# Layer 0's attention: scaling the second product by GpSimd in SBUF instead of by VectorE out of PSUM

## The chip, the cores and the metric

The kernel runs on one core of one Trainium2 chip. The metric is the device time of one execution in microseconds (us); the median of a few runs is compared. The profile is one execution taken apart by the hardware profiler. Its engines are PE (TensorE matmuls), PEld (TensorE weight loads), DVE (VectorE), ACT (ScalarE), POOL (GpSimd) and SP (SyncE, which issues most DMA transfers).

## The reference

Two layers follow each other on x of shape (8, 512, 32, 32): 8 images, 512 channels, T = 1024 pixels, all fp32. Each is a group norm, 1x1 convolutions to q, k and v, softmax attention over the pixels, a 1x1 projection, and the residual sum. Layer 0 has 8 heads of 64 channels, layer 1 one head of 512. The change is in layer 0's attention:

```
h = group_norm(x)
q, k, v = split(w_qkv @ h + b_qkv)            # per head: 64 channels x 1024 pixels
weight = softmax(q^T k / sqrt(64))            # over s, the 1024 source pixels
a[c, t] = sum_s weight[t, s] * v[c, s]
out = x + w_proj @ a + b_proj
```

The kernel leaves the division of the softmax to the end: e = exp(score), a = (sum_s e v) / (sum_s e). So a needs two things for every column t: the unscaled product, and the reciprocal of the column's sum.

## The kernel before, in words

**Work over the images.** One loop runs over the 8 images b. Each pass has the attention of layer 0 for image b (`attention0`, line 395), then a stage of products (v of the next image, projection of this one, q and k of the next), then layer 1 for image b. Products of 512 x 512 by 512 x 1024 are made in seven half-size products instead of eight (`wino`, line 223), for which VectorE makes sums and differences of halves (`left_sums`, `right_sums`; the lines 155 to 158 and 166 to 169). The tiles `t_h` and `h` of the next image get theirs during `attention0`, through the list `extra`; the tile `a` gets its own (`image_factors(a)`, tiles `t_a`) after it.

**attention0.** It handles 8 blocks per image: 4 head pairs `hp`, and for each the two halves `tb` of 512 target pixels. A block has 8 steps s over 128 source pixels each. In a step, TensorE makes the two heads' scores `sc` (128 x 1024 in PSUM, two banks; three such buffers rotate), ScalarE takes the exponential into a tile `e` (line 413), and VectorE adds `e` into the tile `sum` (called `total` in the code; line 415 for the first add, line 417 for six more). Then TensorE makes `av`, the product of `e` with `v`: 16 matmuls into one PSUM bank, head 0 in partitions 0 to 63 and head 1 in 64 to 127.

**reciprocals** (line 366). Four small matmuls with a matrix of ones add `sum` over the partitions (`sums`, in PSUM). VectorE takes the reciprocal `rc` (line 377) and keeps the least one seen (`low_recs`, line 378); GpSimd adds all of them up in `all_recs` (line 379); both serve a check at the kernel's end. The values lie in a compact form, so SP writes them to DRAM as rows (line 381) and reads them back twice, one row for each head, spread over 64 partitions each, into the tile `r` (line 391).

**Scaling.** The function `scaled` multiplies `av`, in PSUM, by `r` and writes `a`:

```python
                    def scaled(hp=hp, tb=tb, av=av, r=r):
                        nc.vector.tensor_mul(a[hp][:, ts(tb, HT)], av, r)
```

It is called in the next block, after that block's adds in the program. The last block's `scaled` is handed to the caller, which calls it in the stage of products.

**Buffers.** `av` and `sums` share a PSUM pool of two banks (`acc_tile`). `rc` and `r` have two SBUF buffers each (`rpool`). A buffer is given out again when its last reader is done.

**Order.** The order of each engine's instructions is fixed at compile time by the tile framework, which plays the program through with a cost model and places what it holds ready; matmuls alone are kept in program order. At run time each engine takes its instructions in that fixed order, each when its semaphores allow.

Of the kernel before, what the change touches and what calls it, by code (L numbers as in the profile page):

```python
# [12 lines left out]
ALU = mybir.AluOpType  # L13
# [15 lines left out]
def two_attention_blocks_kernel(  # L29
# [8 lines left out]
    nc = tc.nc  # L38
    B, C, T = x.shape
    KC = C // P  # L40
    HT = T // 2
# [23 lines left out]
    def matmul(*args, **kw):  # L65
        tc.keep_in_program_order(nc.tensor.matmul(*args, **kw))  # L66
# [105 lines left out]
    def main_path(ctx):  # L172
# [11 lines left out]
        def pair_tile(name):  # L184
            return big_tile(name, (P, 2, HT))

        def acc_tile(name):
            return ps_acc.tile([P, HT], F32, tag="acc", name=name)
# [168 lines left out]
        def channel_tiles(name):  # L357
            return [big_tile(f"{name}_{c}") for c in range(KC)]
# [7 lines left out]
        def reciprocals(total, uid, across):  # L366

            sums = acc_tile(f"sums_{uid}")[:, : 2 * P].rearrange("p (a b) -> p a b", a=2)
            for i in range(4):
                matmul(sums[ts(i, 32), :, :], ones[:, :32], total[:, :, ts(i, P)], start=True, stop=True)
            rc = rpool.tile([P, 2, P], F32, tag="rc", name=f"rc_{uid}")
            nc.vector.reciprocal(rc, sums)  # L377
            nc.vector.tensor_tensor(low_recs, low_recs, rc, ALU.min)
            nc.gpsimd.tensor_tensor(all_recs, all_recs, rc, ALU.add)  # L379
            rows = rowpool.tile([2, 4, P], F32, tag="rows", name=f"rows_{uid}")  # L380
            nc.sync.dma_start(rows.rearrange("j i n -> i j n"), rc[0:P:32, :, :])
            if across:
                r = pair_tile(f"r_{uid}")
                for j in range(2):
                    row = rows[j : j + 1].rearrange("j i n -> j (i n)")
                    nc.sync.dma_start(r[:, j, :], row.to_broadcast([P, HT]))
            else:
                r = rpool.tile([P, HT], F32, tag="r", name=f"r_{uid}")
                for j in range(2):
                    row = rows[j : j + 1].rearrange("j i n -> j (i n)")  # L390
                    nc.sync.dma_start(r[ts(j, 64), :], row.to_broadcast([64, HT]))
            return r


        def attention0(b, q, k, v, extra):
            a = channel_tiles(f"a0_{b}")
            scaled = None
            n = 0
            for hp in range(KC):
                for tb in range(2):  # L400
                    uid = f"0_{b}_{hp}_{tb}"
                    total = pair_tile(f"sum_{uid}")
                    es = []
                    for s in range(NS):
                        sc = ps_pools[n % 3].tile([P, 2, HT], F32, tag="sc", name=f"sc_{uid}_{s}")
                        n += 1
                        for j in range(2):
                            matmul(
                                sc[:, j, :], k[hp][ts(j, 64), ts(s, P)], q[hp][ts(j, 64), ts(tb, HT)],
                                start=True, stop=True,  # L410
                            )
                        e = pair_tile(f"e_{uid}_{s}")
                        nc.scalar.activation(e, sc, AF.Exp, scale=(C // 8) ** -0.5)  # L413
                        if s == 1:
                            nc.vector.tensor_add(total, es[0], e)  # L415
                        elif s > 1:
                            nc.vector.tensor_add(total, total, e)  # L417
                        es.append(e)
                    for f in extra.pop(0) if extra else ():
                        f()  # L420
                    if scaled:
                        scaled()
                    av = acc_tile(f"av_{uid}")
                    for s in range(NS):
                        for j in range(2):
                            matmul(
                                av[ts(j, 64), :], v[s // 2][:, s % 2, hp * P + j * 64 : hp * P + (j + 1) * 64],
                                es[s][:, j, :], start=(s == 0), stop=(s == NS - 1),
                            )
                    for f in extra.pop(0) if extra else ():  # L430
                        f()
                    r = reciprocals(total, uid, False)

                    def scaled(hp=hp, tb=tb, av=av, r=r):
                        nc.vector.tensor_mul(a[hp][:, ts(tb, HT)], av, r)  # L435

            assert not extra
            return a, scaled
# [165 lines left out]
        for b in range(B):  # L604
# [5 lines left out]
            if more:  # L610
# [4 lines left out]
                for i, f in enumerate(steps):  # L615
                    extra[8 + i].append(f)
            psum_pools(f"attention_{b}", 1)
            a, scaled = attention0(b, q, k, v, extra)
            psum_pools(f"products_{b}", 2)

# [309 lines left out]
```

## Time and profile before

| what | value |
| --- | --- |
| time, three runs | 2998.86, 3001.4 and 3006.32 us, median 3001.4 |
| the profiled execution | 3001.43 us; its span, first to last instruction, 2998.6 us |
| granted TensorE clock | 0.994 |
| busy in the span: PE, DVE, ACT, POOL | 98%, 61%, 25%, 4% |
| one block of `attention0` when nothing is late | 14.65 us |
| blocks in the program | 64 (8 images, 8 each) |
| `e` (ACT, line 413) | 512 times, mean 1.051 us |
| `sum` adds (DVE, line 417) | 384 times, mean 1.223 us |
| `a<-av,r` (DVE, line 435) | 64 times, mean 0.686 us |
| `all_recs` add of 128 x 256 (POOL, line 379) | 72 times, mean 0.883 us |

Busy time is a sum over the whole span. A block's 14.65 us are read in the timeline as the distance from its first score matmul to the next block's. The seven windows of the images 2 to 8 from the first score matmul of their attention to the first `sums` matmul of its last block or a little later show 90.5 us of DVE work in about 115 us, 59.5 of ACT and 6.3 of POOL.

### The profile page before, as it was taken

Reading aid. Unit: us, or ns where it says so; the run is one execution under the profiler, and the core shown is the slowest. Engines: PE = TensorE matmul, PEld = TensorE weight load, DVE = VectorE, ACT = ScalarE, POOL = GpSimd, SP = SyncE. Lnnn points to the kernel's source line nnn. Section 1 sums busy time; section 2 is a strip of 40 time slices with the busy share of each in tenths; the row PEclk is TensorE's granted clock in tenths of the full one; section 3 lists DMA queues with packets and bytes.
Section 4 is the critical chain, followed back from the end, with each engine's and each line's share of the span. In section 5 each row is a group of like instructions: output and inputs, shape, how many; then the busy total and the mean of one; then the engine's idle time right before and its main releaser. Section 6 shows DMA issues by size and latency. Waiting matters only on the chain.

```text
span 2998.6 us, 26895 instructions
## 1 busy us (share of the span) xinstructions
PE 2944.2 (98%) x10322; PEld 1409.5 (47%) x10322; DVE 1836.1 (61%) x2445; ACT 754.6 (25%) x925; POOL 112.8 (4%) x119
## 2 busy tenths in 40 slices
PE   7999999999999999999999999999999999999899
PEld 5535454354543545435453354534445354543345
DVE  4376565764667647575466754677546765557745
ACT  1153111421124111341114411143111431214220
POOL 0000000000000000000000000000000000000000
PEclk9999999999999999999999999999999999999899
DMA  7422314023140231402322133411324023030100
GB/s 258 166 80 80 138 60 172 19 92 130 59 169 18 107 142 51 150 27 100 144 101 96 47 115 113 145 46 46 130 105 168 19 76 140 33 144 19 39 0 37
DMA packets 78296, 283.56 MB, mean 95 GB/s; under 512 B 9360, under 2 KB 16336, under 8 KB 71632
## 3 DMA queue, kind: packets, MB, share of 16 engines
q1 hardware_dynamic: 77744, 281.61, 26.3%
q8 instruction: 83, 1.36, 0.2%
q14 instruction: 53, 0.43, 0.0%
q10 hardware_dynamic: 416, 0.16, 0.0%
HBM read 207.51 MB, written 74.22 MB: 94 GB/s over the span
## 4 chain that ended last, share of the span: by engine, by line
PE 84%; DVE 7%; issue 4%; DMA 3%; ACT 1%; SPq 0%; POOL 0%; DVEq 0%; ACTq 0%; POOLq 0%
PE sc L66 9%; PE av L66 8%; PE psb_av L66 5%; PE psb_sc L66 5%; DVE sum L417 5%; PE psa_av L66 4%; PE psc_av L66 4%; PE psc_sc L66 4%; PE psa_sc L66 4%; PE psb_z L66 3%; PE psb_q L66 3%; PE psb_v L66 3%; PE psb_g L66 3%; PE psb_k L66 3%; PE psb_p L66 2%
## 5 line engine op out<-in xcount | busy, mean ns | idle before, releaser
L413 ACT ACTIVATE e<-sc 128x1024 f32<-128x1024 f32 x512 | 476.4, 1051 | 582.7 <-PE sc L66 582.7
L417 DVE TENSOR_TENSOR sum<-sum,e 128x1024 f32<-128x1024 f32 x384 | 469.8, 1223 | 34.5 <-ACT e L413 0.8
L66 PE MATMUL sc<-q_again,k_again 64*128 64x512 f32 x1792 | 399.7, 596 | 0.0
L66 PE MATMUL av<-e,v_again 128*64 128x512 f32 x1792 | 396.9, 595 | 0.0
L66 PEld LDWEIGHTS sc<-q_again,k_again 64*128 64x128 f32 x1792 | 166.7, 186 | 212.2 <-ACT e L413 103.7
L66 PEld LDWEIGHTS av<-e,v_again 128*64 128x64 f32 x1792 | 123.7, 137 | 266.3 <-issue 254.2
L377 DVE RECIPROCAL rc<-sums 128x256 f32<-128x256 f32 x72 | 126.4, 1756 | 80.3 <-PE sums L66 47.7
L379 POOL TENSOR_TENSOR all_recs<-all_recs,rc 128x256 f32<-128x256 f32 x72 | 63.6, 883 | 1611.1 <-DVE rc L377 1611.1
L464 ACT ACTIVATE e<-e 128x512 f32<-128x512 f32 x96 | 60.3, 630 | 238.8 <-DVE e L463 238.8
L66 PE MATMUL psa_sc<-g,h 128*128 128x512 f32 x256 | 115.1, 592 | 0.0
L66 PE MATMUL psa_av<-e,z 128*128 128x512 f32 x256 | 113.2, 595 | 0.0
L415 DVE TENSOR_TENSOR sum<-e,e 128x1024 f32<-128x1024 f32 x64 | 78.4, 1225 | 48.9 <-ACT e L413 48.9
L136 ACT ACTIVATE h<-h,b,s 128x1024 f32<-128x1024 f32 x30 | 36.5, 1238 | 169.3 <-DMA h<-in_x 161.4
L66 PEld LDWEIGHTS psa_sc<-g,h 128*128 128x128 f32 x256 | 48.6, 190 | 61.2 <-issue 61.2
L66 PEld LDWEIGHTS psa_av<-e,z 128*128 128x128 f32 x256 | 48.0, 190 | 54.8 <-issue 50.6
L435 DVE TENSOR_TENSOR a<-av,r 128x512 f32<-128x512 f32 x64 | 43.9, 686 | 46.2 <-DMA r<-rows 46.2
L234 DVE TENSOR_TENSOR u_av<-psb_av,t_av 128x512 f32<-128x512 f32 x16 | 11.1, 691 | 93.1 <-PE psb_av L66 93.1
L66 PE MATMUL psb_p<-t_a,w_p 128*128 128x512 f32 x128 | 60.5, 615 | 5.2 <-DVE t_a L167 5.2
L66 PE MATMUL sums<-sum,ones 128*32 128x256 f32 x576 | 46.0, 391 | 18.1 <-DVE sum L417 17.9
L66 PE MATMUL psa_g<-h,w_m 128*128 128x512 f32 x128 | 60.0, 613 | 3.2 <-ACT h L136 3.2
L66 PE MATMUL sc<-q,k 64*128 64x512 f32 x256 | 59.2, 612 | 0.7 <-ACT e L413 0.7
L66 PE MATMUL psb_z<-w_z,t_h 128*128 128x256 f32 x256 | 58.4, 381 | 0.0
(281 smaller groups left out, 4159.1 us busy)
## 6 DMA issues: line engine op xcount, KB each, us to landing
x<-in_x SPq DMA_DIRECT2D x36, 512.0 KB
h<-in_x SPq DMA_DIRECT2D x32, 512.0 KB
r<-rows SPq DMA_DIRECT2D x128, 128.0 KB
out<-x SPq DMA_DIRECT2D x64, 256.0 KB
w_p<-sums_p SPq DMA_DIRECT2D x8, 1792.0 KB
spill<-v SPq DMA_DIRECT2D x28, 512.0 KB
w_m<-sums_m SPq DMA_DIRECT2D x8, 1792.0 KB
spill<-q SPq DMA_DIRECT2D x28, 512.0 KB
```

The lines of the kernel that those rows point to most:

```text
L66: tc.keep_in_program_order(nc.tensor.matmul(*args, **kw))
L136: nc.scalar.activation(dst, src, AF.Identity, bias=b, scale=s)
L234: nc.vector.tensor_add(t[i], ps["b", i], t1[i])
L377: nc.vector.reciprocal(rc, sums)
L379: nc.gpsimd.tensor_tensor(all_recs, all_recs, rc, ALU.add)
L413: nc.scalar.activation(e, sc, AF.Exp, scale=(C // 8) ** -0.5)
L415: nc.vector.tensor_add(total, es[0], e)
L417: nc.vector.tensor_add(total, total, e)
L435: nc.vector.tensor_mul(a[hp][:, ts(tb, HT)], av, r)
L464: nc.scalar.activation(dst, dst, AF.Exp, scale=scale)
```

## The change

ScalarE copies `av` out of PSUM into `a` as soon as the product is there, unscaled. When `r` has come through DRAM, GpSimd multiplies that half of `a` by `r` in place, in SBUF, for the first seven blocks of an image. For the last block of an image the multiplication stays with VectorE and with the caller, now in place in SBUF. The reciprocals, their rows in DRAM and the loads of `r` stay as they are.

```diff
         def attention0(b, q, k, v, extra):
             a = channel_tiles(f"a0_{b}")
-            scaled = None
             n = 0
...
                     for f in extra.pop(0) if extra else ():
                         f()
-                    if scaled:
-                        scaled()
                     av = acc_tile(f"av_{uid}")
...
                     for f in extra.pop(0) if extra else ():
                         f()
+                    dst = a[hp][:, ts(tb, HT)]
+                    nc.scalar.copy(dst, av)
                     r = reciprocals(total, uid, False)
-
-                    def scaled(hp=hp, tb=tb, av=av, r=r):
-                        nc.vector.tensor_mul(a[hp][:, ts(tb, HT)], av, r)
+                    if (hp, tb) != (KC - 1, 1):
+                        nc.gpsimd.tensor_tensor(dst, dst, r, ALU.mult)
+                    else:
+                        scaled = lambda dst=dst, r=r: nc.vector.tensor_mul(dst, dst, r)
```

## Prediction, made before the result was known

> **What bounds the kernel now.** I read the page's busy table first.
>
> ```profile
> span 2998.6 us, 26895 instructions
> PE 2944.2 (98%) x10322; PEld 1409.5 (47%) x10322; DVE 1836.1 (61%) x2445; ACT 754.6 (25%) x925; POOL 112.8 (4%) x119
> ```
>
> TensorE is busy for 2944.2 us: only 54.4 us are idle, and no change to other engines can win more than that. So the question is which idle time of TensorE the changed multiplication causes. The view of the tile `a` shows how long VectorE stood still in front of it:
>
> ```profile
> L435 DVE TENSOR_TENSOR a<-av,r x64: 678/684/693, 173.9 to 2810.7; 128x512 f32<-128x512 f32 x64
> its engine sat idle before it (us, times) until:
>   DMA r<-rows: 46.2, 27
> ```
>
> Idle VectorE costs nothing by itself. The view of line 417 says who waited for the adds queued behind it:
>
> ```profile
> who waited for it (us, times):
>   PEld sums L66: 39.2, 24
>   PE sums L66: 17.9, 23
> ```
>
> TensorE's `sums` matmuls came late 23 times, 17.9 us in all. The timeline of the fifth block of image 3 shows one such case, VectorE first, then TensorE:
>
> ```profile
> 935.55 1.23 DVE L415 TENSOR_TENSOR sum<-e,e 128x1024 f32<-128x1024 f32 x1 [0.74 <-ACT e L413]
> 936.88 1.23 DVE L417 TENSOR_TENSOR sum<-sum,e 128x1024 f32<-128x1024 f32 x1
> 939.55 0.69 DVE L435 TENSOR_TENSOR a<-av,r 128x512 f32<-128x512 f32 x1 [1.45 <-DMA r<-rows]
> 940.16 5.20 DVE L417 TENSOR_TENSOR sum<-sum,e 128x1024 f32<-128x1024 f32 x4
> 945.28 1.29 DVE L166 TENSOR_TENSOR t_h<-h 128x512 f32<-128x512 f32 x2
> 946.49 1.22 DVE L417 TENSOR_TENSOR sum<-sum,e 128x1024 f32<-128x1024 f32 x1
> ```
>
> ```profile
> 939.47 7.09 PE L66 MATMUL av<-e,v_again 128*64 128x512 f32 x32
> 947.75 0.64 PE L66 MATMUL sums<-sum,ones 128*32 128x256 f32 x8 [1.20 <-DVE sum L417]
> ```
>
> The multiplication was placed behind two adds, its row came 1.45 us too late, five adds stood behind it, and the last ended at 947.71. TensorE had been through with `av` at 939.47 + 7.02 = 946.49 (in a block without delay `sums` starts 7.02 after `av`). The same timeline for all 64 blocks gives a fixed pattern: the start of `sums` less that of `av`, less 7.02, is zero in the blocks 1, 2, 4, 6 and 8 of every image and positive in 3, 5 and 7, where the multiplication sits early; in the others it is the last or last but one before the final add, and the row has long landed. Summed over the images: 4.0 us in the third blocks, 11.0 in the fifth, 4.7 in the seventh, 19.6 together (the 17.9 of the view, with the waits too small for it).
>
> **What the Trainium skill says.** "PSUM — Partial Sum Buffer", section "Engine vs sequencer instructions", has VectorE's, ScalarE's and GpSimd's queues as strict FIFO; the 1.45 us in front of five ready adds agree. "GPSIMD Engine Reference", section 1 "Specifications", gives GpSimd no access to PSUM, which is why the copy must come along. "SBUF — State Buffer", section "Who interferes with whom", says that a VectorE instruction with two SBUF inputs contends with a GpSimd instruction that reads SBUF, and that the one which starts first blocks the other. The timeline agrees where GpSimd happened to be first:
>
> ```profile
> 456.15 0.73 POOL L379 TENSOR_TENSOR all_recs<-all_recs,rc 128x256 f32<-128x256 f32 x1 [42.55 <-DVE rc L377]
> 456.46 0.70 DVE L378 TENSOR_TENSOR low_recs<-low_recs,rc 128x256 f32<-128x256 f32 x1
> ```
>
> The VectorE operation took 0.70 us; its median is 0.424. So it was held 0.28 us, that is until 0.59 after GpSimd's start, 0.14 before GpSimd's end. The adds of line 417 read two SBUF tiles and will meet the new multiplication.
>
> **The change part by part.**
>
> *Removed from VectorE:* 56 multiplications within attention (7 x 8), 0.61 us of its time each (939.55 to the next start at 940.16), and the 46.2 us of waiting less the 5.0 of the very last one, which stays. This is what frees the 19.6 us, if nothing takes its place.
>
> *Added on ScalarE:* 64 copies of 128x512 from PSUM. The nearest row is the copy `t_k<-psa_k` of line 245, same shape, mean 586 ns: 37.5 us. It waits for the end of `av`; behind it stand the next block's exponentials, which need scores that start 0.57 us after `sums`. The timeline of ScalarE has a hole there in every block:
>
> ```profile
> 918.98 7.44 ACT L413 ACTIVATE e<-sc 128x1024 f32<-128x1024 f32 x8 [7.53 <-PE sc L66]
> 933.57 7.44 ACT L413 ACTIVATE e<-sc 128x1024 f32<-128x1024 f32 x8 [7.16 <-PE sc L66]
> ```
>
> `av` ends near 931.8, the copy by 932.6, the next exponential starts at 933.57. Cost nothing, hidden by the scores; bounds 0 and, if it ever stood behind an exponential, 0.6 us of three score buffers' lead, also nothing. No gain either: TensorE never waited for the bank of `av`.
>
> *Added on GpSimd:* 56 multiplications of 128x512 with two SBUF inputs. No such row. From below: 0.73 us for 256 columns with the ports free, and the slope from "GPSIMD Engine Reference", section 3.1 (4497 ns for 2048 columns): (4497 - 727) / 1792 = 2.10 ns a column, so 727 + 256 x 2.10 = 1.27 us. From above: twice 727, 1.45 us. Less the 0.14, VectorE is held H = 1.13 to 1.31 us by each, and I take 1.2. It cannot be a gain; it can be zero if GpSimd only gets in when VectorE pauses. The multiplication waits for `r`, as before 5 to 6 us after `rc`, the middle of the adds. Behind it on GpSimd is only the next `all_recs` add, a block later, and after the stage the norm of line 138 and the power of line 125, tens of us later. Who waits for it: `t_a` (lines 166 to 169) after attention, and the buffer of `r`, needed two blocks on.
>
> *DMAs:* none added or removed; SP's three issues for each block keep their place, and POOL issues none. The bank of `av` comes free 10 us sooner; nobody waits for it. The last multiplication of an image stays on VectorE, 0.68 us from SBUF as from PSUM; for image 8 TensorE's wait of 5.2 us behind it stays.
>
> *What VectorE's slack pays.* After the change, with no hold, the final add ends ahead of TensorE's need by: in the blocks 2, 3, 4, 7 some 1.9 us (block 4 of image 3 ended 1.27 early with a multiplication of 0.61 in it); in block 5, 946.49 - (947.71 - 0.61 - 1.45) = 0.84, less 0.04 for the hand-over, 0.80, because two `t_h` operations stand before the final add; in the blocks 6 and 8, about 0.7 + 0.6 = 1.28. Image 8 has no `t_h` and 1.9 everywhere. Each image then loses (H - 0.80) in block 5, twice (H - 1.28) in 6 and 8, four times (H - 1.9), where positive. For H = 1.13: 7 x 0.33 = 2.3 us; for 1.31: 7 x (0.51 + 0.06) = 4.0; I take 3.1.
>
> *Sum:* 19.6 - 3.1 = 16.5 us gained: span 2998.6 - 16.5 = 2982.1. The profiled run was 3001.43 us, practically the median 3001.4 of the three, which differ by 7.5 us; so 3001.4 - 16.5 = 2984.9.
>
> **The rivals.** (a) *GpSimd hides wholly:* it gets the ports only in the pause after the final add, or its hold is under 0.8. Then all 19.6 us come back: 2981.8. For it: VectorE's adds are close together, pitch 1.31 for 1.22. Against: the same lock held VectorE at 456.46. (b) *Slower: the multiplication holds VectorE twice,* in front of two adds, H = 2.25, because its two input streams take turns at the ports. Place: the adds of every block from the second on. Loss 7 x (1.45 + 2 x 0.97 + 4 x 0.35) + 7 x 0.35 = 36 us, less 19.6: 3017.8. It decides from H = 1.95, where losses reach 19.6. Against: 0.59 us of hold for 256 columns would have to become nearly four times that for 512. (c) *The compiler reorders:* the time freed on VectorE in its plan pulls the second `t_h` operation of the blocks 6 and 8 in front of the final add (0.6 us less slack, 0.68), or H is 1.65. Loss at H = 1.2: 7 x (0.4 + 2 x 0.52) = 10.1, at 1.65 with the old order 7 x (0.85 + 2 x 0.37) = 11.1: 2991.9 to 2992.9. (d) *The change doesn't take effect:* a GpSimd instruction or a copy that the program names cannot be left out; but the freed time may be filled with other work that waits, and the time stays near 3001.
>
> **How the numbers follow.** A measurement can tell about 0.3% of this kernel, 9 us, from no change: 2992.4 and 3010.4 are the bounds. The forecast has 0.55, (a) 0.15, (c) 0.12, half of it beyond 2992.4, (d) 0.05, (b) 0.13. Faster is 0.55 + 0.15 + 0.06 = 0.76, same 0.11, slower 0.13. The range runs from 2980, a little under (a), to 3000, beyond (c); it leaves out (b), (d) and little else.
>
> **What would show it.** In the changed profile: no wait of DVE for `r` but the last ones; `sums` waits of PE on line 417 falling from 17.9 to some 3 us, all in fifth blocks; copies of `av` at 0.59 us ahead of the first exponential; POOL multiplications of 1.3 to 2.5 us (some of it waiting) 5 to 6 us after `rc`; one add in each block at 2.3 instead of 1.22 us. A POOL multiplication above 2.5 us, two lengthened adds in a block, or `sums` waits in blocks 2 and 4 would make the prediction wrong.

## The result, and the profile after

The changed kernel took 2982.97 us (median of 4 runs, 2981.65 to 2986.85), the kernel before in 4 runs 3002.36 us: ratio 0.9937, 95% interval 0.992 to 0.9954. Measured twice more beside the experiments, the ratio was 0.9954 (0.994 to 0.9968) and 0.9948 (0.9934 to 0.9961). The medians differ by 13 to 19 us in the three pairs; 16.5 were forecast. The profiled execution took 2986.85 us.

The head of the page after the change:

```profile
span 2985.1 us, 27085 instructions
PE 2945.3 (99%) x10322; PEld 1412.5 (47%) x10322; DVE 1854.3 (62%) x2389; ACT 791.9 (27%) x989; POOL 220.5 (7%) x175
```

TensorE's busy time is the same within 1.1 us; what shrank is its idle time (span less busy time), from 54.4 to 39.8 us. VectorE has 56 instructions less and is busy 18 us longer. The view of the adds (line 416 now) says who waited for them:

```profile
who waited for it (us, times):
  PEld sums L66: 48.7, 54
  PE sums L66: 1.4, 7
```

The PE row fell from 17.9 to 1.4 us. The PEld row is no measure of lateness: it counts the 0.81 us that weight loading pauses ahead of every `sums`, as soon as an add is the last thing it waited for (in the run no_mult below it has 11.4 us in 14 waits, and nothing is late there). The timeline of the 64 blocks (start of `sums` less start of `av` less 7.02, added up; lateness from here on) gives 4.7 us against 19.6, and 4.3 and 4.4 in the two later profiles of the same kernel. Not one of the blocks 3 and 7 is late any more; the blocks 5, 6 and 8 of the images 1 to 7 are late by 0.21 each, two of them by 0.37 and 0.38.

The fifth block of image 3 again, VectorE, then GpSimd, then TensorE, then ScalarE (the 16 matmuls of `av` and the 4 of `sums` in the program are 32 and 8 records in the trace):

```profile
933.30 7.43 DVE L416 TENSOR_TENSOR sum<-sum,e 128x1024 f32<-128x1024 f32 x5
940.65 1.29 DVE L166 TENSOR_TENSOR t_h<-h 128x512 f32<-128x512 f32 x2
941.85 1.22 DVE L416 TENSOR_TENSOR sum<-sum,e 128x1024 f32<-128x1024 f32 x1
```

```profile
936.27 2.05 POOL L433 TENSOR_TENSOR a<-a,r 128x512 f32<-128x512 f32 x1 [4.46 <-DMA r<-rows]
```

```profile
935.89 7.09 PE L66 MATMUL av<-e,v_again 128*64 128x512 f32 x32
943.12 0.64 PE L66 MATMUL sums<-sum,ones 128*32 128x256 f32 x8
```

```profile
928.37 0.58 ACT L430 COPY a<-av 128x512 f32<-128x512 f32 x1 [5.59 <-PE av L66]
930.00 7.44 ACT L412 ACTIVATE e<-sc 128x1024 f32<-128x1024 f32 x8 [1.04 <-PE sc L66]
```

GpSimd now waits for the row, and VectorE passes by. The five adds take 7.43 us instead of the 6.54 of five adds in a row in the kernel before, because one of them is held: GpSimd's work beside it makes it longer. The final add ends at 943.07, where TensorE is through with `av` at 935.89 + 7.02 = 942.91; `sums` starts at 943.12, 0.21 late instead of 1.26. ScalarE's copy is done 1.04 us before the next exponential starts. The held add and the one before it, each seen alone in a narrow window of the timeline:

```profile
935.96 1.23 DVE L416 TENSOR_TENSOR sum<-sum,e 128x1024 f32<-128x1024 f32 x1
937.29 2.11 DVE L416 TENSOR_TENSOR sum<-sum,e 128x1024 f32<-128x1024 f32 x1
```

### The profile page after: what moved, and what is told of

Read it like the earlier page. It is cut to its first block, busy times and chain, and to the rows that moved or that the text cites. A ratio compares the mean times of both kernels' runs of the same rounds, so it can differ in the third digit from the quotient of the medians.

```text
span 2985.1 us, 27085 instructions
## 1 busy us (share of the span) xinstructions
PE 2945.3 (99%) x10322; PEld 1412.5 (47%) x10322; DVE 1854.3 (62%) x2389; ACT 791.9 (27%) x989; POOL 220.5 (7%) x175
## 5 line engine op out<-in xcount | busy, mean ns | idle before, releaser
L416 DVE TENSOR_TENSOR sum<-sum,e 128x1024 f32<-128x1024 f32 x384 | 519.8, 1354 | 40.3 <-DVE sum L416 1.4
L430 ACT COPY a<-av 128x512 f32<-128x512 f32 x64 | 37.5, 585 | 356.8 <-PE av L66 356.8
L433 POOL TENSOR_TENSOR a<-a,r 128x512 f32<-128x512 f32 x56 | 108.1, 1930 | 258.2 <-DMA r<-rows 229.2
L136 ACT ACTIVATE h<-h,b,s 128x1024 f32<-128x1024 f32 x30 | 36.5, 1238 | 171.1 <-DMA h<-in_x 138.1
L125 POOL TENSOR_TENSOR rstd<-ve,mhalf 128x4 f32<-128x4 f32 x16 | 16.3, 1018 | 610.5 <-DVE ve L123 610.5
```

The source lines that it names most:

```text
L125: nc.gpsimd.tensor_tensor(rstd, ve, mhalf, ALU.pow)
L136: nc.scalar.activation(dst, src, AF.Identity, bias=b, scale=s)
L430: nc.scalar.copy(dst, av)
L433: nc.gpsimd.tensor_tensor(dst, dst, r, ALU.mult)
```

## The experiments

Theory: VectorE takes its instructions in order; the multiplication waited there for a row still on its way through DRAM, with ready adds behind it, and the last add holds TensorE's `sums`. Taking that wait off VectorE's queue is the gain; GpSimd's reads give a part of it back. Rivals: VectorE's freed work (56 x 0.61 us) is the gain; or the earlier release of PSUM by the copy is. The diffs are excerpts: those of order_only and copy_only are against the kernel before, that of old_row shows what it adds to copy_only, and that of twice is against the changed kernel. `tc.issue_after(x)` places what its block issues behind `x` in the queue of `x`'s engine; `tc.keep_in_program_order` pins an instruction's place.

The lateness is read from the profile of each run. Taken from TensorE's idle time, it leaves 33.4 to 36.5 us in the kernel before (34.8), the changed one (35.1) and every other run but old_row (31.1). So what these edits change in TensorE's idle time is, to within some 4 us, the lateness of `sums`.

**order_only.** Only the place of the multiplication in VectorE's queue is changed. (In the order that came of it, the second `t_h` operation of the blocks 6 and 8 also stands in front of the final add, as in the changed kernel.)

```diff
-                            nc.vector.tensor_add(total, total, e)
+                            final = nc.vector.tensor_add(total, total, e)
...
                     if scaled:
-                        scaled()
+                        with tc.issue_after(final.ins):
+                            scaled()
```

> The kernel before, with one thing changed: VectorE's multiplication out of PSUM stays, but in every block it is issued behind the block's final add. No copy, nothing new on GpSimd, no VectorE work removed. Theory (the gain comes from taking the wait for the reciprocals' row out from in front of the adds): TensorE's sums waits on line 417 fall from 17.9 us to under 3, time 2979 to 2985 us. Rival 1 (VectorE's freed 0.61 us in each block is the gain): no gain, about 3002. Rival 2 (the earlier release of the av bank by ScalarE's copy is the gain): about 3002 or slower, since the bank is now held longer.

2979.82 us beside 2997.36 for the kernel before, ratio 0.9943 (0.9929 to 0.9956). The same block:

```profile
935.23 1.28 DVE L166 TENSOR_TENSOR t_h<-h 128x512 f32<-128x512 f32 x2
936.43 1.22 DVE L417 TENSOR_TENSOR sum<-sum,e 128x1024 f32<-128x1024 f32 x1
937.56 0.68 DVE L436 TENSOR_TENSOR a<-av,r 128x512 f32<-128x512 f32 x1
```

The multiplication follows the final add and no longer waits; no block is late. All of VectorE's work is still there and the bank of `av` is held longer, and yet the whole lateness is gone: both rivals fall.

**copy_only.** ScalarE copies, VectorE multiplies in SBUF in the next block, where the compiler puts it.

```diff
+                    dst = a[hp][:, ts(tb, HT)]
+                    nc.scalar.copy(dst, av)
                     r = reciprocals(total, uid, False)
...
-                    def scaled(hp=hp, tb=tb, av=av, r=r):
-                        nc.vector.tensor_mul(a[hp][:, ts(tb, HT)], av, r)
+                    def scaled(dst=dst, r=r):
+                        nc.vector.tensor_mul(dst, dst, r)
```

> One part of the change alone: ScalarE copies av out of PSUM into a, and VectorE multiplies it in place in SBUF in the next block, where the planner puts it (behind the second add of the blocks 2 to 8, now in all of them). Theory: the wait for the row stands in front of the adds in seven blocks of eight, sums waits of 15 to 25 us, time 2997 to 3007. Rival 2 (releasing the PSUM bank is the gain): about 2983. Rival 1 (VectorE's work): about 3002.

3028.71 us, ratio 1.0107 (1.0092 to 1.0123): slower than before, by more than expected. Two views, the idle time of VectorE in front of the multiplication and those who waited for the adds:

```profile
DVE a L437 <- DMA r<-rows: 94.5, 57, 4.8
```

```profile
who waited for it (us, times):
  PEld sums L66: 90.9, 56
  PE sums L66: 40.6, 48
```

With the copy, the compiler puts the multiplication behind the second add in the blocks 2 to 8 of every image, not in three of them (in block 2 of image 1 alone behind the fourth). The wait doubled from 46.2 to 94.5 us and the lateness from 19.6 to 45.3. The mechanism and the place are the ones expected; my figure of 15 to 25 us stayed at the size of the kernel before, although four more blocks of each image are late. The lateness rose by 25.7 us and the profiled spans differ by 26.4 (3025.0 against 2998.6); the timed runs say 31, see under twice.

**old_row.** copy_only with the multiplication pinned behind the second add and `r` of the block before, which landed long ago; `r` has three buffers instead of two for that. VectorE's order in the 64 blocks is that of copy_only but for block 2 of image 1. This changes the scale of layer 0's product.

```diff
-                    r = reciprocals(total, uid, False)
+                    row = reciprocals(total, uid, False)
+                    r, landed = (landed or row), row
...
+                            if s == 3:
+                                tc.keep_in_program_order(add)
+                            elif s == 2 and scaled:
+                                tc.keep_in_program_order(scaled())
```

> The kernel copy_only with the same order on VectorE (the multiplication behind the second add of the blocks 2 to 8), but multiplying by the row of reciprocals of the block before, which has landed long ago (the first block of an image keeps its own). The scale of layer 0's product is thereby another. The work and its place are the same as in copy_only, the wait alone is gone. Theory (the wait is what delays the adds): lateness of the sums falls from 45 us to under 6 us (what is left in block 2 and some hundredths in blocks 5, 6 and 8), time within 5 us of order_only, about 2980. Rival (VectorE work in front of the adds is enough): 3010 to 3029.

2984.12 us beside 3001.81, ratio 0.9944 (0.9931 to 0.9958). VectorE's waits for the row fell from copy_only's 94.5 us to those for the first row of each image:

```profile
  DMA r<-rows: 16.1, 8
```

The lateness is 6.5 us (under 6 were expected), all of it in the second blocks, where the first block's multiplication still waits for its own row; image 1 has most of it, 4.1 us, where the row came 5.27 us late. The other blocks are not late at all, although the multiplication stands in front of five adds as in copy_only. So neither the place nor the work, but the wait at that place costs the time.

**copy_behind.** copy_only with the `issue_after` of order_only.

> The kernel copy_only with the multiplication issued behind the block's final add. Theory: the copy costs nothing and the place of the wait everything, so the same as order_only, 2977 to 2983 us, no lateness. Rival (the copy, or reading a in SBUF, costs by itself): 3000 to 3029.

2982.19 us beside 3001.81, ratio 0.9936 (0.9923 to 0.995), no lateness. ScalarE's copies cost nothing that can be seen.

**no_mult.** The changed kernel without `nc.gpsimd.tensor_tensor(dst, dst, r, ALU.mult)`: it leaves out the scaling of seven blocks in eight.

> The changed kernel without GpSimd's multiplications: in seven blocks of eight the second product of layer 0 stays unscaled (that part of the computation is left out). Shows what the multiplication still costs on GpSimd. Theory: the remaining lateness of the sums, 4.7 us in the changed kernel's timeline, goes, and nothing else: about 2978 us. Rival (the rest of the lateness comes from the t_h operations alone): 2983.

2979.22 us beside 3000.25, ratio 0.9931 (0.9917 to 0.9944), no lateness; the changed kernel beside it (after_again) had 2986.95, 1 us above its expected range, and 0.9954. Without GpSimd's multiplications the 4.3 to 4.7 us of lateness that remain after the change are gone.

> The changed kernel once more, beside the following ones on the same chip: 2981 to 2986 us.

**twice.** The changed kernel, with a second GpSimd multiplication.

```diff
                         nc.gpsimd.tensor_tensor(dst, dst, r, ALU.mult)
+                        extra_t = rpool.tile([P, HT], F32, tag="x", bufs=1, name=f"x_{uid}")
+                        tc.keep_in_program_order(nc.gpsimd.tensor_tensor(extra_t, dst, r, ALU.mult))
```

> The changed kernel with a second GpSimd multiplication of the same two tiles into a scratch tile right behind the first, 56 times. Theory (each GpSimd multiplication holds VectorE's adds for 0.885 us, which is paid in the blocks 5, 6 and 8 of seven images, where two t_h operations stand in front of the final add): the sums come later by 0.88 in these 21 blocks, 18.6 us more than the changed kernel, about 3001 us; blocks 2, 3, 4 and 7 have 1.9 us of slack and just bear 1.77. Rival (GpSimd's work is hidden whatever it is): about 2983. A hold that counts in every block would give 2983 + 49 x 0.88 = 3026.

3009.87 us beside 2997.36, ratio 1.0043 (1.0029 to 1.0056), where about 3001 was expected: the hold can eat the gain. The adds as one group (busy us, mean ns | idle before), in the kernel before, in the changed kernel and then in this one:

```profile
L417 DVE TENSOR_TENSOR sum<-sum,e 128x1024 f32<-128x1024 f32 x384 | 469.8, 1223 | 34.5 <-ACT e L413 0.8
```

```profile
L416 DVE TENSOR_TENSOR sum<-sum,e 128x1024 f32<-128x1024 f32 x384 | 519.8, 1354 | 40.3 <-DVE sum L416 1.4
```

```profile
L416 DVE TENSOR_TENSOR sum<-sum,e 128x1024 f32<-128x1024 f32 x384 | 568.2, 1480 | 40.3 <-DVE sum L416 1.4
```

Busy time is 469.8 without GpSimd's multiplications, 519.8 with one, 568.2 with two in each block but the last: 50.0 and 48.4 more, or 0.89 and 0.86 us for each multiplication. The lateness rose to 26.5, in the blocks 5, 6 and 8 by 6.1 to 6.3 us each (7 x 0.885 is 6.2), as expected, and by 3.0 in the blocks 2, 3, 4 and 7, whose slack was just used up. It explains 7 us over the kernel before, and the profiled spans differ by 7.5; the timed runs say 12.5 (9 to 17). The rest lies in the executions that were profiled: that of the kernel before took 3001.43 us, 4 more than its median beside these runs, and that of this kernel 3007.84, 2 less than its own. Why the kernel before took 4 us less beside these runs is open, since it was not profiled there.

**write_only.** As twice, but with `nc.gpsimd.memset(extra_t, 0.0)` for the second multiplication.

> The changed kernel with a GpSimd memset of a 128x512 scratch tile right behind each of the 56 multiplications: GpSimd work at the same place that reads nothing from SBUF. Theory (only GpSimd's reads hold VectorE's adds with two SBUF inputs): no lengthened adds beyond one in each block, about 2983 us. Rival (any GpSimd instruction holds VectorE): some 0.5 us more in 21 blocks, about 2993.

2986.16 us, ratio 0.9959 (0.9945 to 0.9972), lateness 4.6. The adds and the memset:

```profile
L416 DVE TENSOR_TENSOR sum<-sum,e 128x1024 f32<-128x1024 f32 x384 | 519.5, 1353 | 40.3 <-DVE sum L416 1.4 <-DVE sum L414 0.9 <-ACT e L412 0.8
...
L435 POOL MEMSET x<- 128x512 f32 x56 | 29.2, 521 | 0.0
```

The adds are no longer than in the changed kernel (519.8), although 55 of the 56 memsets fall beside one, and no memset takes more than 0.53 us. GpSimd's reading holds them, its writing doesn't. The Trainium skill ("SBUF — State Buffer", section "Who interferes with whom") says just that of VectorE instructions with two SBUF inputs, and these numbers agree.

**th_behind.** The changed kernel, with the `t_h` operations issued behind the final add: `with tc.issue_after(final.ins):` around both loops over `extra.pop(0)`. In image 1 the list `extra` also holds the preparation of weights (`prepare_p`, `prepare_m`, `prepare_z`), which moves with them into the blocks 1 to 3.

> The changed kernel, with the t_h operations on VectorE issued behind each block's final add instead of in front of it. GpSimd's hold stays. Theory (hold and t_h together overrun the slack, neither alone): lateness goes, about 2978 us. Rival (the hold alone overruns it): 2983.

2982.43 us beside 3000.25, ratio 0.9936 (0.9922 to 0.9949), no lateness, though its adds are held as before (mean 1348 ns). The time is 4.5 us below after_again's beside it; by itself it lies nearer the rival's 2983 than the theory's 2978, and it is the profile that decides. As no_mult, with the `t_h` operations in front but no hold, has no lateness either, hold and `t_h` overrun the slack only together.

**both_behind.** The kernel before with both, order_only's multiplication and th_behind's `t_h` operations.

> The kernel before, with VectorE's multiplication out of PSUM and the t_h operations both issued behind each block's final add; no copy, no GpSimd multiplication. Theory (order on VectorE is all that matters): no lateness of the sums, about 2978 us, as good as the changed kernel with the same order of t_h. Rival (the relief by GpSimd is needed, since VectorE's pause of 1.9 us plus 0.64 for the sums can't take 1.8 us of work before the next reciprocal): 2985 or more.

2987.47 us beside 3000.25, ratio 0.9956 (0.9942 to 0.997), not the 2978 that I expected. Images 2 to 8 have no late block; the 4.1 us of lateness are all in image 1. The rest of the miss is not lateness: in this profile TensorE is busy for 2946.4 us at a granted clock of 0.991, in th_behind's for 2944.5 at 0.992. The rival's figure, 2985 or more, came true, but its reason, too much VectorE work in the pause, makes no block of the images 2 to 8 late. TensorE in image 1:

```profile
197.00 0.96 PE L66 MATMUL sums<-sum,ones 128*32 128x256 f32 x8 [2.12 <-DVE a L438]
```

The multiplication waits 2 us for its row there even behind the final add. Then `sums` waits for the bank of the `av` of the block before, which the multiplication has not yet read out. The row's way in the trace, from SP's queue:

```profile
183.60 0.57 SPq L381 DMA_DIRECT2D rows<-rc  x1
187.64 0.32 SPq L297 DMA_DIRECT2D w_p<-sums_p  x1
188.01 1.11 SPq L391 DMA_DIRECT2D r<-rows  x2
```

The moved preparation of weights has put `w_p<-sums_p` in front of the row's reads, and it waits 3.4 us for `sums_m`. So `r` is issued 4.41 us after `rows`; in order_only it is 1.67 (177.50 and 179.17). From that issue to the multiplication's start at 196.25 it is another 8.2 us, with the 1792 KB of `w_p` issued just ahead; in the changed kernel, where no weights move in that block, it is 3.5 (182.40 to 185.91). A wait in front of ready work again, in another queue, and brought in by the edit itself. In th_behind `r` is issued as late, and VectorE's order in image 1 is the same but for the multiplication, yet nothing is late: ScalarE's copy has freed the bank. That is the one place in these runs where freeing PSUM early is worth something.

**order_again** and **after_third**, on one chip:

> The kernel order_only again, beside the changed kernel on one chip. Its profile shows no lateness of the sums, the changed kernel's 4.3 to 4.7 us: 3 to 6 us below it.

> The changed kernel beside order_again: 2981 to 2987 us, 3 to 6 us above it.

2982.98 and 2984.71 us beside 3001.81, ratios 0.9939 (0.9925 to 0.9952) and 0.9948 (0.9934 to 0.9961). The profiles show no lateness and 4.4 us; the times differ by 1.7 us where 3 to 6 were expected, and the intervals overlap. By time alone, order_only can't be told from the changed kernel. Several versions (order_only, copy_behind, th_behind) have no late block and lie at 0.9936 to 0.9943, the changed kernel at 0.9937 to 0.9954: a reordering alone is as good as the change.

## Why the prediction was right, step by step

- *What bounds it, and the 19.6 us to be had:* right, and shown by order_only, copy_behind and no_mult, which get all of it back in their profiles.
- *The removed wait is the gain, not the removed work:* right; old_row and copy_only have the same work in the same place, one without the wait, one with it.
- *ScalarE's copy costs nothing:* right (585 ns each, 1.04 us of pause behind it; copy_behind). No run has GpSimd read PSUM, so that the copy was needed is not shown here. That an earlier free bank brings nothing is right for the changed kernel, but both_behind shows a case where it would.
- *GpSimd's multiplication, 1.27 us at the least:* right; the shortest took 1.269 us, the median 2.000 with its waiting. 55 adds are held, in the median 2.11 us long, no two in one block.
- *The hold H of 1.13 to 1.31 us:* too large. It is 0.885 (2.11 us less the usual 1.225; 0.86 to 0.89 from the groups). I let the whole 1.27 us, less 0.14 at the end, fall on VectorE. In the block shown, GpSimd's instruction starts at 936.27 while an add runs that ends at 937.19, and it ends itself at 938.32, 1.13 us after that add. The held add takes 0.885 more than the usual 1.225, so VectorE goes on at 938.18, 0.14 before GpSimd's end, as forecast. It would have paused 0.10 between two adds anyway: 1.13 - 0.14 - 0.10 = 0.89. The other 0.14 of GpSimd's 1.27 us must have run beside the add before; that part is worked out, not measured by itself.
- *Slack of the blocks:* too large as well. In no_mult, which has the changed kernel's order on VectorE and no hold, the final add of image 3 ends 0.73 us ahead of TensorE's need in the blocks 5, 6 and 8 and 1.74 in 2, 3, 4 and 7, each before the 0.04 to 0.05 of hand-over; I had 0.84 in block 5, some 1.3 in 6 and 8, and 1.9. For 6 and 8 I had taken one `t_h` operation in front of the final add, as in the kernel before; in the new order both stand there, so these two behave like block 5. This is what rival (c) says happens; its reason, time freed on VectorE in the plan, is not shown, for order_only frees none and has both there too.
- *The loss of 3.1 us:* near the 4.3 to 4.7 measured, in three blocks of an image instead of one, and by luck. With the hold alone put right, the forecast's own sum gives 7 x (0.885 - 0.80) = 0.6 us; with the slack alone put right, 7 x 3 x (1.2 - 0.68) = 10.9, close to rival (c)'s 10.1. The two errors cancel nearly; with both put right it is 7 x 3 x (0.885 - 0.68) = 4.3.
- *Rival (b), a double hold that makes it slower:* not so for one multiplication, but twice shows the point. With 2 x 0.885 = 1.77 us of hold in each block the kernel was slower than before; the threshold had been put at 1.95, with the larger slacks.

## What to carry to other kernels

On an engine that takes its instructions in order, an instruction that waits for a round trip through DRAM belongs behind the work that others need next, or on an engine on which nothing stands behind it. Before moving such work to another engine, try moving it in its own queue: here that gave the same. An operation moved to GpSimd is not free for VectorE: count its SBUF reads as a hold on VectorE's adds of two SBUF tiles (0.885 us here for a multiplication that takes 1.27 alone), and compare the hold with the slack of the tightest block.

## What the runs showed that I had not expected

The same multiplication, fed from SBUF instead of PSUM and otherwise unchanged in the program, was put by the compiler behind the second add in seven blocks instead of three, and made the kernel 1% slower (copy_only). The place was known before that run, the size of the loss was not. In both_behind, moving a list of operations on VectorE changed the order of SP's queue as well. The order that a planner gives is part of the cost of any edit.
